# Where the residual is added in a graph-network kernel: in an accumulating output scatter, or on VectorE from a sorted copy, with other lead times in the plan

## The chip, the cores and the metric

The kernel runs on one core of one Trainium2 chip. The metric is the device time of one execution in microseconds (us). Engine names are those of the profile: PE is TensorE (PEld its weight loads), DVE is VectorE, ACT is ScalarE, POOL is GpSimd and SP is the engine whose queue issues the plain transfers.

## The reference

Sixteen graphs of 1024 nodes with 64 channels go through two layers. The first normalises each node's channels, multiplies by the dense adjacency matrix divided by its row sums, and adds the result to `x`. The second thins each node's list of neighbours, takes three quantiles over the remaining neighbours channel by channel (a sort of each list), passes the weighted sum through two small matrix products and adds that.

```python
h = jnp.maximum(_layernorm(x, axis=-1), 0.0)
x = x + _L0_gnn_ref(h, adj)                    # (adj / row sums) @ h
h = jnp.maximum(_layernorm(x, axis=-1), 0.0)
x = x + _L1_gnn_ref(h, adj, nodemask, W1, b1, W2, b2)

# inside _L1_gnn_ref
adj_d = _dilate_adj(adj, mask)                 # drops some neighbours
agg = _weighted_nanquantile_agg(x, adj_d > 0)  # quantiles 0.25, 0.5, 0.75
out = x + agg
h = relu(out @ W1 + b1)
y = h @ W2 + b2
return y * mask[..., None]
```

## The kernel before

The first layer works graph by graph. Eight row blocks of 128 nodes are loaded (`at`), their signs taken on ACT (`sg`), neighbours listed on DVE (`rec`), the blocks transposed on PE (`pt`, copied to `att`) and multiplied with the normalised nodes (`products`). The result, the input plus the messages, lies in the tile `row` in its columns from `X1`. The stream `channels` normalises it, stores it with SP to the output `out` (line 708) and the normalised channels to a table `tab` in DRAM. The stream `endings` sorts the nodes by the length of their lists: each of eight indirect DMAs per graph scatters 128 rows of `row`, without the part from `X1`, to their sorted places in `srt` in DRAM (line 775).

Four graphs make a group of 32 tiles of 128 nodes with lists of like length. One `Job` takes a class of tiles: lists of 15, 10, 8, 7 (two tiles), 6, 5 (four), 4 (four), 3 (six), 2 (six) and 1 (five). It gathers each neighbour's channels from `tab` with one indirect DMA per tile and list place (`places`, four buffers), loads the nodes' own channels from `srt` into `S`, sorts the places on DVE in place and in PSUM (`other`), weighs them (`prod`, two buffers), and then runs `layers`: PE transposes and adds the weighted places (`pt`), ACT copies (`ot`), PE multiplies by `W1` (`ph`), ACT applies the bias and relu (`hid`), PE multiplies by `W2` and adds the second bias by a product with a row of ones (`py`), and ACT multiplies by the mask (`y`). At most four tiles share one `py`, so that there are 56 such groups in the whole kernel. Last, one indirect DMA per tile adds 128 rows of `y` to the output in DRAM (line 1012). The very long lists of the first tile of each group are done together by `long_lists`, with up to 88 gathers per tile (`lplaces`), as four more jobs. So there are 16 x 8 = 128 row scatters (`srt<-row`) and 128 output scatters (`out_dram<-y`).

The order of work on DVE and POOL is written out when the program is built, by the class `Plan`. The work is a set of generators. Each yields the engine that it needs next and a time at which its operands should be there, and the plan picks the one that can begin first by its own prices. These times only set the order of instructions: on the chip each engine takes its queue in order and waits for semaphores. Margins are added to the operands' times:

```python
BREATH = 0.8
AHEAD = 16
SLACK = 2.0
LOOSE = 7.0
```

An indirect DMA costs 1.27 us in the plan, whatever it does, and its data are ready 2.2 us later (line 292); a memset on POOL costs 0.15. Every scatter that directly follows one of the same kind is preceded by a memset of `turn` (line 788). `room(name, bufs)` is the time at which the oldest buffer of a tile comes free. Of the program's engines only DVE and POOL keep the plan's order by hand; the tile framework orders the others. If a list is longer than its class allows, a flag `go` starts a dense path instead, which these inputs don't need.

Of the kernel before, what the change touches and what calls it, by code (L numbers as in the profile page):

```python
# [9 lines left out]
F32 = mybir.dt.float32  # L10
# [4 lines left out]
AF = mybir.ActivationFunctionType  # L15
OP = mybir.AluOpType
AX = mybir.AxisListType

P = 128
# [192 lines left out]
AHEAD = 16  # L212
SLACK = 2.0
LOOSE = 7.0


class Timed:
# [13 lines left out]
class Plan:  # L231
# [24 lines left out]
    def room(self, name, bufs):  # L256

        tiles = self.slots.get(name, ())
        if len(tiles) < bufs:
            return 0.0  # L260
        old = tiles[-bufs]
        return INF if self.users[old] else max(self.used.get(old, 0.0), self.ready.get(old, 0.0))

    def at(self, *tiles):
        return max(self.ready.get(t.tensor.name, INF) for t in tiles)
# [98 lines left out]
def list_path(ctx, tc, x, adj, nodemask, w1, b1, w2, b2, out, go):  # L364
# [9 lines left out]
    W = C + 2  # L374
    PW = W // 2
    REC = 8 * NSEG + 2
    R0 = W
    X1 = RW = R0 + REC
    NTAU = N // SUB
    NF = NG + NG + len(LONG)  # L380

# [58 lines left out]
    nc.sync.dma_start(w2_sb, w2)  # L440
    b1_sb = consts.tile([H, 1], F32, name="b1_sb")
    nc.sync.dma_start(b1_sb, b1.rearrange("(h o) -> h o", o=1))
    b2_sb = consts.tile([1, CO], F32, name="b2_sb")
    nc.sync.dma_start(b2_sb, b2.rearrange("(o c) -> o c", o=1))
    taus = consts.tile([P, len(QUANTILES)], F32, name="taus")
    for k, (tau, wt) in enumerate(QUANTILES):
        nc.vector.memset(taus[:, k:k + 1], tau)
# [107 lines left out]
    def beginnings(pool, now):  # L555

        for b, st in enumerate(batch):
            now[0] = b
            yield "DVE", lambda: max(known(st, "xt", "mrow"), room("h0", 3), room("row", 4))
            mrow_f = new(tiny, [NT, P], F32, "mrow_f", 2)  # L560
            nc.vector.tensor_copy(mrow_f, st["mrow"])

            h0 = new(pool, [P, NT, C + 1], F32, "h0", 3, users=2)
            nc.vector.memset(h0[:, :, C:], 1.0)
            row = st["row"] = new(pool, [P, NT, X1 + C], F32, "row", 4, users=1)
            nc.vector.memset(row[:, :, C:W], -1.0)
            yield from normed(h0[:, :, :C], st["xt"])
            st["h0"] = h0
            yield "PE", lambda: max(at(mrow_f), room("ps_small", 3))
            pm = new(ps_s, [P, HALF], F32, "ps_small", 3, users=1)  # L570
            nc.tensor.transpose(pm[:, :NT], mrow_f, ident[:NT, :NT])
            yield "ACT", lambda: at(pm)
            nc.scalar.copy(row[:, :, RW - 1], pm[:, :NT])
            nc.scalar.copy(row[:, :, RW - 2], row_f)
            free(pm)
# [79 lines left out]
    def products(pool, now):  # L655


        for b, st in enumerate(batch):
            now[0] = b
            for hf in range(2):  # L660
                yield "PE", lambda: INF if st["copied"][hf] < 2 * BPH else max(
                    at(st["att"][hf]), known(st, "h0"), room("ps_small", 3)
                )
                po = new(ps_s, [P, HALF], F32, "ps_small", 3, users=1)
                for q in range(NT):
                    if q and q % 2 == 0:
                        yield "PE", always
                    nc.tensor.matmul(
                        po[:C + 1, :], st["h0"][:, q, :], st["att"][hf][:, q, :],
                        start=(q == 0), stop=(q == NT - 1),  # L670
                    )
                free(st["att"][hf])
                free(st["h0"])
                yield "ACT", lambda: max(at(po), room("msg", 2))
                msg = new(pool, [C + 1, HALF], F32, "msg", 2)
                nc.scalar.copy(msg, po[:C + 1, :])
                free(po)
                yield "PE", lambda: max(at(msg), room("ps_small", 3))
                pb = new(ps_s, [P, HALF], F32, "ps_small", 3, users=1)
                sums = pb[:, :BPH * (C + 1)].rearrange("p (k c) -> p k c", c=C + 1)  # L680
                for k in range(BPH):
                    nc.tensor.transpose(
                        sums[:, k, :], msg[:, k * P:(k + 1) * P], ident[:C + 1, :C + 1]
                    )
                yield "DVE", lambda: at(pb) + SLACK
                x1 = st["row"][:, hf * BPH:(hf + 1) * BPH, X1:]
                deg = new(tiny, [P, BPH], F32, "deg", 2)
                nc.vector.tensor_scalar(deg, sums[:, :, C], 1.0, None, op0=OP.max)
                nc.vector.reciprocal(deg, deg)
                nc.vector.tensor_tensor(  # L690
                    x1, sums[:, :, :C], deg.unsqueeze(2).to_broadcast([P, BPH, C]), OP.mult
                )
                nc.vector.tensor_tensor(
                    x1, x1, st["xt"][:, hf * BPH:(hf + 1) * BPH, :], OP.add
                )
                free(pb)
                st["residual"] += 1
            free(st["xt"])

    def channels(pool, now):  # L700

        for b, st in enumerate(batch):
            now[0] = b
            row = lambda: st["row"]
            yield "DVE", lambda: known(st, "row") if st["residual"] == 2 else INF
            yield from normed(row()[:, :, :C], row()[:, :, X1:])

            nc.sync.dma_start(out[b].rearrange("(t p) c -> p t c", p=P), row()[:, :, X1:])
            nc.sync.dma_start(
                tab[b * TS:b * TS + N, :].rearrange("(t p) w -> p t w", p=P), row()[:, :, :W]  # L710
            )
            st["normed"] = True

    def endings(pool, now):

        first = lambda rank: rank - 3000
        for b, st in enumerate(batch):
# [53 lines left out]
            to = new(pool, [P, NT], I32, "to", 2)  # L771
            nc.vector.scalar_tensor_tensor(to, low, float(1 - GB), pos, op0=OP.mult, op1=OP.add)
            for t in range(NT):
                yield "POOL", lambda: max(at(to), at(row)) + LOOSE if "normed" in st else INF, first
                scatter(srt[g], row[:, t, :RW], to[:, t:t + 1], sorts[g])
            free(row)
            progress["batches"] = b + 1

# [4 lines left out]
            in_offset=bass.IndirectOffsetOnAxis(ap=idx, axis=0),  # L783
        )

    def scatter(dst, src, idx, others, op=OP.bypass):
        if plan.last is others:
            nc.gpsimd.memset(turn, 0.0)
        ins = nc.gpsimd.indirect_dma_start(
            out=dst, out_offset=bass.IndirectOffsetOnAxis(ap=idx, axis=0),  # L790
            in_=src, in_offset=None, compute_op=op,
        )

        for other in others:
            tc.declare_no_dep(ins.ins, other, reason="rows of their own")
        others.append(ins.ins)
        plan.last = others

    class Job:
# [8 lines left out]
        def run(self):  # L808
# [9 lines left out]
            progress["ahead"] += T * (n - 1)  # L818
            if short:
                mine = self.S  # L820
                self.S = new(pool, [P, T, W], F32, "S", 4, users=1)
                nc.sync.dma_start(self.S, mine)
            for t in range(T):
                for k in range(n - 1):
                    if t or k:
# [2 lines left out]
                    gather(A[:, k + 1, t, :], self.table, self.idx[:, t, k:k + 1])  # L828
                    progress["ahead"] -= 1
            yield "DVE", lambda: max(  # L830
                at(A, self.S) + SLACK, room("prod", 2) if short else 0.0,
                room("other" if short else "long_other", 1),
            ), self.later
            yield from self.sort()
# [129 lines left out]
        def layers(self, terms, sources):  # L964

            T, R = self.T, terms[0][0].shape[1]
            yield "PE", lambda: max(at(*sources) + LOOSE, room("y", 4), room("pt", 2))
            y = new(mlp, [P, T, CO], F32, "y", 4, users=1)
            for t0 in range(0, T, 4):
                ts = range(t0, min(t0 + 4, T))  # L970
                M = len(ts) * P
# [23 lines left out]
                yield "PE", lambda: max(at(hid) + SLACK, room("ps_small", 3))  # L995
                py = new(ps_s, [P, HALF], F32, "ps_small", 3, users=1)
                pv = py[:, :len(ts) * CO].rearrange("p (t c) -> p t c", c=CO)
                for i, t in enumerate(ts):
                    nc.tensor.matmul(
                        pv[:, i, :], hid[:, i * P:(i + 1) * P], w2_sb, start=True, stop=False  # L1000
                    )
                    nc.tensor.matmul(pv[:, i, :], ones_f[:1, :], b2_sb, start=False, stop=True)
                yield "ACT", lambda: at(py) + SLACK
                for i, t in enumerate(ts):
                    nc.scalar.activation(
                        y[:, t, :], pv[:, i, :], AF.Copy, scale=self.mask[:, t:t + 1]
                    )
                free(py)
            for t in range(T):
                yield "POOL", lambda: at(y) + LOOSE  # L1010
                rows = out_rows[:min(self.g + 1, NG) * GB * N, :]
                scatter(rows, y[:, t, :], self.nodes_i[:, t:t + 1], scatters, OP.add)
            free(y)
            progress["jobs"][self.g] += 1

    def group(g):
# [107 lines left out]
        for i, ts in enumerate(classes):  # L1124
            n, T = CAPS[ts[0]] + 1, len(ts)
            sl = slice(ts[0], ts[-1] + 1)
            job = Job(
                gat, n, T, keys[:, sl, :n - 1], idx[:, sl, :], node[:, sl], mask[:, sl],
                nodes_i[:, sl], table, tiles[:, sl, :W], g,
            )  # L1130
            plan.add(job.run(), 100 * g + i)
        progress["groups"] = g + 1
# [393 lines left out]
```

## Time and profile before

| what | value |
|---|---|
| median of 3 runs | 1586.0 us (1583.88 to 1586.02) |
| the profiled execution | 1823.34 us |
| its span | 1821.4 us |
| TensorE clock granted in it | 0.653 |
| busy in the span: DVE, POOL, PE, ACT | 1240.1, 1050.8, 825.6, 609.3 us |

A group of the profile names the output and the inputs of an instruction by the program's names, its shapes and count, its busy time and the mean of one. After the bar stands the idle time of the engine just before those instructions and what ended it. "issue" is idle time in which the profile shows nothing that was waited for. Nearly all instructions carry line 225, that of a helper which records every operation for the plan, so tiles tell them apart. For an indirect DMA the POOL time is that of the instruction on POOL; the data move on the DMA engines beside it.

### The profile page before, as it was taken

How to read it: one execution, taken by the hardware profiler on the slowest of the kernel's cores; microseconds unless marked ns; L12 is line 12 of the kernel's file. 1: busy time of each engine (PE TensorE's matmuls, PEld its weight loads, DVE VectorE, ACT ScalarE, POOL GpSimd, SP SyncE). 2: the span in 40 equal slices, each digit the busy share in tenths (PEclk: the TensorE clock that was granted, in tenths of full speed). 3: DMA queues.
4: the chain of work that ended last, by engine and by line, in shares of the span. 5: the costliest groups of instructions: out<-in, count | busy, mean ns of one | idle time of the engine just before them, and what ended most of it. 6: DMA issues, size and time to landing. Idle time of an engine off the chain costs nothing. (4 is left out here: it accounts for less than half of the span.)

```text
span 1821.4 us, 15210 instructions
## 1 busy us (share of the span) xinstructions
PE 825.6 (45%) x3336; PEld 533.0 (29%) x3336; DVE 1240.1 (68%) x4046; ACT 609.3 (33%) x1874; POOL 1050.8 (58%) x1144
## 2 busy tenths in 40 slices
PE   5767822365686572563685000110031366253364
PEld 3333411233444341232354000100021245242343
DVE  7865858475788486678642889339497678896622
ACT  8877653245655464444442000000010111010011
POOL 0112263636467655555758766567656788575757
PEclk8978855675798675775885555555555567555656
DMA  5544741233444353353222211101111112111112
GB/s 170 163 133 122 199 125 31 48 101 81 121 134 112 58 134 91 90 138 73 56 48 49 43 43 34 23 17 22 28 24 28 18 26 20 23 30 23 24 18 17
DMA packets 147941, 124.89 MB, mean 69 GB/s; under 512 B 117715, under 2 KB 117843, under 8 KB 147843
## 3 DMA queue, kind: packets, MB, share of 16 engines
q1 hardware_dynamic: 102818, 86.58, 16.8%
q0 software_dynamic: 45024, 37.28, 12.2%
q14 instruction: 71, 0.57, 0.1%
q8 instruction: 28, 0.46, 0.1%
HBM read 104.51 MB, written 19.28 MB: 68 GB/s over the span
## 5 line engine op out<-in xcount | busy, mean ns | idle before, releaser
L225 POOL DMA_INDIRECT places<-tab,idx x496 | 495.0, 998 | 165.1 <-issue 140.2
L225 PE MATMUL pt<-ident,prod 128*128 128x128 f32 (+1 forms) x736 | 161.8, 384 | 569.4 <-DVE prod L225 294.5
L225 POOL DMA_INDIRECT out_dram<-y,nodes_i x124 | 208.0, 1678 | 186.8 <-ACT y L225 127.4
L225 PEld LDWEIGHTS pt<-ident,prod 128*128 128x128 f32 (+1 forms) x736 | 134.2, 267 | 605.3 <-issue 389.7
L225 POOL DMA_INDIRECT srt<-row,to x128 | 129.4, 1011 | 259.0 <-ACT row L225 223.5
L225 PE MATMUL pt<-ident,at 128*128 128x128 f32 x1024 | 190.0, 334 | 179.6 <-ACT att L225 72.1
L225 PE MATMUL ps_small<-att,h 128*65 128x512 f32 x512 | 259.0, 652 | 17.7 <-ACT h L225 10.3
L225 PEld LDWEIGHTS pt<-ident,at 128*128 128x128 f32 x1024 | 143.5, 171 | 236.5 <-ACT att L225 97.7
L225 POOL DMA_INDIRECT lplaces<-tab,lidx x163 | 171.0, 1049 | 49.7 <-issue 49.1
L225 ACT COPY att<-pt 128x512 f32<-128x512 f32 x256 | 142.9, 583 | 155.7 <-remote 84.2
L225 DVE MAX8 rec<-sg 128x8 f16<-128x256 f16 x512 | 180.1, 414 | 9.5 <-remote 5.2
L225 ACT ACTIVATE wu<-wu 128x39 f32<-128x39 f32 (+9 forms) x40 | 9.4, 234 | 431.7 <-DVE wu L225 168.8
L225 ACT ACTIVATE sg<-at 128x1024 f16<-128x1024 f32 x128 | 134.9, 1055 | 31.7 <-DMA at<-in_adj_dram 15.3
L225 DVE TENSOR_TENSOR sg<-sg,keyed 128x1024 f16<-128x1024 f16 x128 | 87.4, 683 | 65.5 <-issue 33.4
L225 PEld LDWEIGHTS ps_small<-att,h 128*65 128x65 f32 x512 | 75.4, 153 | 149.4 <-issue 126.5
L225 ACT COPY ot<-pt 128x128 f32<-128x128 f32 (+3 forms) x56 | 22.4, 400 | 246.7 <-remote 128.2
L225 PE MATMUL ps_small<-ot,w_sb 128*128 128x128 f32 (+3 forms) x112 | 55.9, 593 | 104.7 <-ACT ot L225 72.6
L225 PE MATMUL ps_small<-w_sb,hid 128*128 128x64 f32 x256 | 72.5, 376 | 52.6 <-ACT hid L225 25.1
L225 DVE TENSOR_TENSOR other<-places,other 128x64 f32<-128x64 f32 (+6 forms) x204 | 69.5, 341 | 35.6 <-remote 16.3
L225 PEld LDWEIGHTS ps_small<-w_sb,hid 128*128 128x128 f32 x256 | 53.6, 258 | 80.5 <-ACT hid L225 40.3
L225 DVE TENSOR_TENSOR rem<-places,recs 128x30 f32<-128x30 f32 (+9 forms) x40 | 7.3, 182 | 101.7 <-DMA places<-tab,idx 90.0
L225 POOL MEMSET turn<- 128x1 f32 x204 | 76.2, 373 | 0.1
(206 smaller groups left out, 1712.2 us busy)
## 6 DMA issues: line engine op xcount, KB each, us to landing
at<-in_adj_dram SPq DMA_DIRECT2D x128, 512.0 KB
places<-tab,idx POOLq DMA_INDIRECT x496
tab<-row SPq DMA_DIRECT2D x16, 264.0 KB
xt<-in_x_dram SPq DMA_DIRECT2D x16, 256.0 KB
out_dram<-row SPq DMA_DIRECT2D x16, 256.0 KB
lplaces<-tab,lidx POOLq DMA_INDIRECT x163
recs<-srt SPq DMA_DIRECT2D x4, 544.0 KB
srt<-row,to POOLq DMA_INDIRECT x128
```

The costliest lines, as they stand in the source:

```text
L225: ins = getattr(self._engine, op)(*args, **kwargs)
```

## The change

The sorted rows now carry the first layer's result as well: `row` is laid out as channels, two markers, `x1`, and then the list record, and all of it is scattered to `srt` (656 bytes a row instead of 400). The store of `out` in `channels` goes. In `layers`, a short job loads the tiles' `x1` from `srt` into `y` (five buffers instead of four) at its start; a long job has it in its own `S`. The second bias goes into PSUM with one product for up to four tiles, ahead of the products with `W2`. The step from `py` to `y` moves from ACT to DVE, which multiplies by the mask and adds `x1` in one instruction a tile. The output scatter becomes a plain one.

In the plan, the new DVE step stands 7 us behind `py` (ACT's stood 2 behind), the output scatters 15 us behind `y` (7 before), the sort of a job 7 us behind its gathers and `S` (2 before), and the row scatters of all graphs but the first four 15 us behind their operands (7 before). `S` of a short job holds 64 columns instead of 66.

```diff
+WIDE = 15.0
...
-    R0 = W
-    X1 = RW = R0 + REC
+    X1 = W
+    R0 = X1 + C
+    RW = R0 + REC
...
-    b2_sb = consts.tile([1, CO], F32, name="b2_sb")
-    nc.sync.dma_start(b2_sb, b2.rearrange("(o c) -> o c", o=1))
+    b2_sb = consts.tile([1, 4 * CO], F32, name="b2_sb")
+    for k in range(4):
+        nc.sync.dma_start(b2_sb[:, k * CO:(k + 1) * CO], b2.rearrange("(o c) -> o c", o=1))
...
-            nc.sync.dma_start(out[b].rearrange("(t p) c -> p t c", p=P), row()[:, :, X1:])
...
-                yield "POOL", lambda: max(at(to), at(row)) + LOOSE if "normed" in st else INF, first
-                scatter(srt[g], row[:, t, :RW], to[:, t:t + 1], sorts[g])
+                yield "POOL", lambda: max(at(to), at(row)) + (LOOSE if b < GB else WIDE) if "normed" in st else INF, first
+                scatter(srt[g], row[:, t, :], to[:, t:t + 1], sorts[g])
...
-            in_=src, in_offset=None, compute_op=op,
+            in_=src, in_offset=None,
...
-                self.S = new(pool, [P, T, W], F32, "S", 4, users=1)
-                nc.sync.dma_start(self.S, mine)
+                self.S = new(pool, [P, T, C], F32, "S", 4, users=1)
+                nc.sync.dma_start(self.S, mine[:, :, :C])
+                self.residual = mine[:, :, X1:R0]
...
-                at(A, self.S) + SLACK, room("prod", 2) if short else 0.0,
+                at(A, self.S) + LOOSE, room("prod", 2) if short else 0.0,
...
-            yield "PE", lambda: max(at(*sources) + LOOSE, room("y", 4), room("pt", 2))
-            y = new(mlp, [P, T, CO], F32, "y", 4, users=1)
+            yield "PE", lambda: max(at(*sources) + LOOSE, room("y", 5), room("pt", 2))
+            y = new(mlp, [P, T, CO], F32, "y", 5, users=1)
+            x1 = y
+            if self.short:
+                nc.sync.dma_start(x1, self.residual)
+            else:
+                x1 = self.S[:, :, X1:R0]
...
+                nc.tensor.matmul(
+                    py[:, :len(ts) * CO], ones_f[:1, :], b2_sb[:, :len(ts) * CO],
+                    start=True, stop=False,
+                )
                 for i, t in enumerate(ts):
                     nc.tensor.matmul(
-                        pv[:, i, :], hid[:, i * P:(i + 1) * P], w2_sb, start=True, stop=False
+                        pv[:, i, :], hid[:, i * P:(i + 1) * P], w2_sb, start=False,
+                        stop=(i == len(ts) - 1),
                     )
-                    nc.tensor.matmul(pv[:, i, :], ones_f[:1, :], b2_sb, start=False, stop=True)
-                yield "ACT", lambda: at(py) + SLACK
+                yield "DVE", lambda: at(py) + LOOSE
                 for i, t in enumerate(ts):
-                    nc.scalar.activation(
-                        y[:, t, :], pv[:, i, :], AF.Copy, scale=self.mask[:, t:t + 1]
+                    nc.vector.scalar_tensor_tensor(
+                        y[:, t, :], pv[:, i, :], self.mask[:, t:t + 1], x1[:, t, :],
+                        op0=OP.mult, op1=OP.add,
                     )
...
             for t in range(T):
-                yield "POOL", lambda: at(y) + LOOSE
-                rows = out_rows[:min(self.g + 1, NG) * GB * N, :]
-                scatter(rows, y[:, t, :], self.nodes_i[:, t:t + 1], scatters, OP.add)
+                yield "POOL", lambda: at(y) + WIDE
+                scatter(out_rows, y[:, t, :], self.nodes_i[:, t:t + 1], scatters)
...
-                nodes_i[:, sl], table, tiles[:, sl, :W], g,
+                nodes_i[:, sl], table, tiles[:, sl, :R0], g,
```

More of the change, by code (lines that the diff above doesn't have):

```diff
@@ L564, in beginnings @@
             nc.vector.memset(h0[:, :, C:], 1.0)
-            row = st["row"] = new(pool, [P, NT, X1 + C], F32, "row", 4, users=1)
+            row = st["row"] = new(pool, [P, NT, RW], F32, "row", 4, users=1)
             nc.vector.memset(row[:, :, C:W], -1.0)
@@ L685, in products @@
                 yield "DVE", lambda: at(pb) + SLACK
-                x1 = st["row"][:, hf * BPH:(hf + 1) * BPH, X1:]
+                x1 = st["row"][:, hf * BPH:(hf + 1) * BPH, X1:R0]
                 deg = new(tiny, [P, BPH], F32, "deg", 2)
@@ L705, in channels @@
             yield "DVE", lambda: known(st, "row") if st["residual"] == 2 else INF
-            yield from normed(row()[:, :, :C], row()[:, :, X1:])
-            nc.sync.dma_start(out[b].rearrange("(t p) c -> p t c", p=P), row()[:, :, X1:])
+            yield from normed(row()[:, :, :C], row()[:, :, X1:R0])
             nc.sync.dma_start(
@@ L784, in gather, with scatter @@
         )
-    def scatter(dst, src, idx, others, op=OP.bypass):
+    def scatter(dst, src, idx, others):
         if plan.last is others:
```

## The prediction

> **What bounds the kernel now.** I read the stage table first (busy us of each engine in a stretch, with instruction counts), because the kernel has two halves. Up to about 1000 us the first layer runs on all engines; after it only the second layer's gathers, sorts and small matmuls are left.
>
> ```profile
> 0.00:1000.00 1000.00, 596.29 (x2365) 352.18 (x2365) 675.77 (x2255) 547.43 (x1675) 496.70 (x608) 0.73 0.40 104
> 1000.00:1822.00 822.00, 229.33 (x973) 180.79 (x972) 564.31 (x1791) 61.87 (x199) 554.13 (x537) 0.56 0.16 26
> ```
>
> Columns after the width: PE, PEld, DVE, ACT, POOL, TensorE clock, DMA share, GB/s. In the second half DVE (564) and POOL (554) look equally loaded, and DMA (0.16) and ACT (62) are out of it. So I asked for POOL's groups in that stretch alone (busy, mean ns, then the idle time just before them).
>
> ```profile
> L225 POOL DMA_INDIRECT places<-tab,idx x241 | 244.8, 1016 | 74.6 <-issue 66.4 <-DMA places<-tab,idx 4.6 <-DMA tab<-drop,didx 1.4
> L225 POOL DMA_INDIRECT lplaces<-tab,lidx x163 | 171.0, 1049 | 49.7 <-issue 49.1 <-DMA lplaces<-tab,lidx 0.6
> L225 POOL DMA_INDIRECT out_dram<-y,nodes_i x70 | 120.4, 1720 | 110.4 <-ACT y L225 77.2 <-ACT prod L225 21.1 <-issue 11.2
> L225 POOL DMA_INDIRECT out_dram<-y,lnodes_i x4 | 6.5, 1626 | 5.3 <-ACT wu L225 4.4 <-issue 0.9
> ```
>
> A fixed gap ("issue") follows each gather, so 404 gathers occupy POOL's queue for 244.8+171.0+74.6+49.7 = 540 us. The 74 output scatters hold it for 127 busy + 12 issue = 139 us, and for 77.2+21.1+4.4 = 103 us more POOL stands at a scatter whose `y` isn't there, with the next gathers queued behind it. Together 782 of 822 us: POOL's queue, waits included, is full. DVE isn't: of its 258 idle us these three are the waits for gathers, 118 us.
>
> ```profile
> DVE rem L225 <- DMA places<-tab,idx: 80.3, 8, 25.0
> DVE lrem L225 <- DMA lplaces<-tab,lidx: 26.9, 1, 26.9
> DVE rem L225 <- issue: 11.1, 3, 8.5
> ```
>
> POOL in order of time shows the price of one scatter and one wait near the end (start, us, [idle before]), and the plain scatters of rows at the first half's end:
>
> ```profile
> 1742.99 1.50 POOL L225 DMA_INDIRECT places<-tab,idx  x1 [0.30 <-issue]
> 1756.50 1.62 POOL L225 DMA_INDIRECT out_dram<-y,nodes_i  x1 [12.01 <-ACT y L225]
> 1795.46 1.57 POOL L225 DMA_INDIRECT out_dram<-y,nodes_i  x1 [0.19 <-issue]
> 1797.34 1.57 POOL L225 DMA_INDIRECT out_dram<-y,nodes_i  x1 [0.19 <-issue]
> ...
> 980.80 0.97 POOL L225 DMA_INDIRECT srt<-row,to  x1 [0.19 <-issue]
> 981.77 0.12 POOL L225 MEMSET turn<- 128x1 f32 x1
> 982.08 0.96 POOL L225 DMA_INDIRECT srt<-row,to  x1 [0.19 <-issue]
> ```
>
> Start to start, an accumulating scatter takes 1797.34-1795.46 = 1.88 us, a plain one 982.08-980.80 = 1.28 us, each with its memset. The planner (line 292) prices both alike, at 1.27 + 0.15.
>
> **What the Trainium skill says.** "Perfetto Trace Analysis", section "DMA Instruction — SWDGE (GPSIMD)": the end of such an instruction is the last descriptor written, not the data's arrival. So 1.57 against 0.97 is work on POOL itself; the trace agrees, since the next POOL instruction starts right after it. "DMA: Bandwidth & Descriptors", section "Rules for kernel authors": an accumulating DMA reads its destination and writes it later, and must wait for other accesses of those bytes. The kernel before does so (the `out` store ahead of the scatters); no wait for that store appears in POOL's list, so dropping it is worth nothing by itself. "Perfetto Trace Analysis", section "Optimizing Scalar/DVE Operations": about 125 ns fixed for DVE on PSUM, 60 on SBUF. The trace has 424 ns for 128x256 from PSUM (`row<-ps_small,deg`) and 430 from SBUF (`row<-row,xt`): no such difference in the profiled durations.
>
> **The change part by part** (us of the profiled execution, which took 1823.3 with a span of 1821.4; the median of the runs is 1586.0, so a saving is scaled by 0.87. The profiled execution is slower by 237 us, and no view says where).
>
> 1. *Plain instead of accumulating scatters.* 74 in the second half x (1.88-1.28) = 44. The last 17 are bound by `y` in the end: it is ready at 1805.3 and the last scatter starts at 1812.4, 7 to be won of 10, so 41. The 54 in the first half free 54x0.60 = 32 of POOL, where it waits for ACT and DVE anyway (in 200 to 1000 us 78 for `row`, 50 for `y`, 24 for `nodes_i`): taken 0, ends 0 and 32.
>
> 2. *Scatters planned 15 instead of 7 us behind `y`.* Only the order on POOL changes: more gathers stand ahead of each scatter, none waits on purpose. The 13 waits of the second half are 10.6, 12.9, 14.0, 7.2, 12.3, 4.4, 10.5, 5.7, 11.3, 12.0, 1.5 and two near nothing. Eight us off each leaves 28 of 103, so 75 at most. But `y` now passes DVE's queue, planned 7 us behind its PSUM tile, and what is late there stays late: I take half, 37; ends 0 and 103. Late next are DVE's step on `py` and the sorts behind it.
>
> 3. *Bias once per group.* 256 bias records of 379 ns become 112 wider ones (56 groups; 128x256 records elsewhere take 580 ns). It moves ahead of `hid`, where PE stands idle, and for four tiles 4x0.62 = 2.5 us leave the path to `y` (pairs start 0.62 apart at the clock of 0.5). Against waits that item 2 cut already: 5; ends 0 and 20.
>
> 4. *Last step on DVE.* No row has a scalar_tensor_tensor of 128x64 from PSUM. Nearest is tensor_tensor `other<-S,places` 128x64 with PSUM output, about 0.22 us; the page's 125 ns plus 64/0.96 = 67 ns gives an estimate of 0.19. I take 0.23, ends 0.15 and 0.31 (ACT's time for it). Second half: 74x0.23 = 17, hidden in DVE's gather waits but for 4; cover gone, 23. First half: 54x0.23 = 12 on the busiest engine: 6 lost, ends 0 and 17. ACT loses 128x0.313 = 40 us; it is off the path in the second half, so 0 taken, up to 10 gained in the first.
>
> 5. *The new wait on DVE.* Behind a step on `py` stand sorts, and in the first half also the layer norms and the listing; `room("places")` makes POOL wait for those sorts. First half: POOL's 7 waits for `y` there came to 50; if all pass to DVE, 50 are lost, if the planned 7 us hold, 0. I take 8. The second half's share is in item 2, and its extreme is the rival below.
>
> 6. *SP.* 16 stores of 0.43 go, 40 loads of `x1` into `y` of 0.37 come, and 3 bias loads of about 0.38 ahead of the first `at`: 1 lost at the start. A load of `y` waits for the scatter of five jobs ago and holds back `at` loads behind it; they run up to five tiles ahead: 0 taken, ends 0 and 15 lost.
>
> 7. *Sorts 5 us and late row scatters 8 us further back.* Both change only order. The first can take 5 us from each of the 12 gather waits (118) while POOL stays the bound: 0 taken, ends 20 gained, 10 lost. The second could delay the last group's start by its 8 us; gathers of group 2 cover that: 0, ends 10 gained, 8 lost.
>
> 8. *Wider sorted rows* (656 instead of 400 bytes). Gathering `adj` rows of 4096 bytes takes POOL 1.00 us, of 264 bytes 0.94 to 1.0, so its time doesn't follow bytes; the DMA share leaves room: 0.
>
> Sum: 41 + 37 + 5 - 4 - 6 - 8 - 1 = **64**. 1823.3 - 64 = 1759.3, or 0.9649; times 1586.0 is **1530**.
>
> **The rivals.**
> *Everything lines up:* with scatters costing what the planner assumes, POOL no longer slips behind it, and all 103 us of waiting go; half of the 32 counts too. 41+103+16+5 less 15 for DVE is 150, scaled 131: **1455**. For it: the waits are of the size of the slip, 74x(1.88-1.42) = 34 us by the end. Against: PE runs at half clock, slower than planned.
>
> *DVE becomes the bound (slower):* the wait for `y` moves onto it. Its slot lies 7 us behind `py`, POOL's lay some 9 behind it, so the same 13 waits would cost 103+13x2 = 129. Second half: 564 busy + 17 + 129 + its 140 idle us that have nothing to do with gathers = 850 against 822, even if no gather is ever late; with 20 lost in the first half, 48, scaled 42: **1628**. It decides from where DVE's waits for `py` and gathers together pass 822-564-17-140 = 101 us. Against it: the planner places that step 7 us late where ACT's had 2, and ACT's order, which often held `ot` up behind `wu`, gets shorter.
>
> *The change gives back what it gains:* POOL empties sooner but `places` has four buffers, and the sorts that release them come later: **1586**. Against it: in the list of waits no gather waits long for a sort (6.1 us is the longest).
>
> **How the numbers follow.** 0.2% (3 us) is about what a measurement of this kernel can tell from no change. POOL's queue shortens: 0.58, own range 1490 to 1570 (items 2 and 5 between a quarter and three quarters of their ends). All waits go: 0.18. DVE the bound: 0.17. Given back: 0.07, of which 0.03 faster, 0.03 same, 0.01 slower. Faster 0.79, same 0.03, slower 0.18. Leaving out the best third of the second case and half of the third, the range is 1440 to 1605.
>
> **What would show it.** Right: the output scatter at 0.97 us and a start-to-start of 1.28; POOL's waits at it under 60 us after 1000; the second half some 70 us shorter, the first within 20. Item 4 is right if the new DVE group has 0.15 to 0.31 us. DVE's idle time before it tells item 5: under 60 us in all for my case, over 100 in the second half for the slower one. Wrong altogether if the scatter keeps its 1.6 us, or if the first half grows by over 30.

## The result and the profile after

The changed kernel took 1579.08 us (median of six runs, 1575.99 to 1583.16), the kernel before beside it 1585.32 (six runs, 1583.88 to 1587.35). The ratio is **0.9962**, with a 95% interval of 0.9946 to 0.9977: a gain of 6 us, where 56 were forecast.

The same program runs at one of two paces: on five chips the kernel before took 1587 to 1589 us and on three others 1851 to 1856, so every ratio below is against runs of the kernel before beside it, and traces are compared at one pace only. The timed runs above are of the first pace. The profile that the prediction was read from (1823 us) was of the second. For the comparison I therefore use another profiled execution of the kernel before, of 1587.6 us (span 1585.7); the changed kernel's has a span of 1576.7.

First the groups of the page that the change touches: busy us, mean ns, then idle time before. The kernel before:

```profile
L225 POOL DMA_INDIRECT out_dram<-y,nodes_i x124 | 207.5, 1673 | 68.2 <-ACT y L225 35.0
L225 POOL MEMSET turn<- 128x1 f32 x204 | 76.5, 375 | 0.1
L225 ACT ACTIVATE y<-ps_small,recs 128x64 f32<-128x64 f32 x124 | 31.3, 313 | 88.3 <-PE ps_small L225 88.1
```

The changed kernel:

```profile
L226 POOL DMA_INDIRECT out_dram<-y,nodes_i x124 | 128.9, 1039 | 55.3 <-DVE y L226 20.2
L226 DVE SCALAR_TENSOR_TENSOR y<-ps_small,recs,y 128x64 f32<-128x64 f32 x124 | 28.2, 275 | 61.7 <-PE ps_small L226 61.7
```

The store did become cheap: 1039 instead of 1673 ns, and POOL's busy time fell from 1061.8 to 980.5 us. But DVE now stands idle for 61.7 us in front of its new step, until the matmul (`py`, in `ps_small`) is done. Before, ACT waited there, for 88.1 us.

The stretch from 800 us to the end, where only the second layer is left, in the table by stage (PE, PEld, DVE, ACT, POOL). Before:

```profile
800.00:1600.00 800.00, 244.24 (x1052) 194.14 (x1052) 571.18 (x1816) 70.21 (x223) 591.65 (x576) 0.57 0.20 29
```

After:

```profile
800.00:1600.00 800.00, 212.25 (x966) 167.21 (x966) 591.39 (x1902) 50.45 (x141) 545.21 (x583) 0.57 0.16 32
```

The kernels end at 1585.7 and 1576.7, so the stretch is really 785.7 and 776.7 us long. POOL is relieved by 46 us in it, DVE loaded by 20. DVE is idle for 785.7 - 571.2 = 214.5 us before and 185.3 after. What it waits for there, before:

```profile
DVE rem L225 <- DMA places<-tab,idx: 62.8, 7, 20.7
DVE lrem L225 <- DMA lplaces<-tab,lidx: 38.7, 2, 36.1
DVE rev L225 <- DMA srt<-row,to: 21.4, 1, 21.4
```

And after (us in total, times, longest):

```profile
DVE y L226 <- PE ps_small L226: 61.4, 16, 7.3
DVE lrem L226 <- DMA lplaces<-tab,lidx: 55.7, 1, 55.7
DVE rem L226 <- DMA places<-tab,idx: 15.9, 2, 9.6
```

The waits for POOL's short gathers shrink from 62.8 to 15.9 us. The faster POOL alone doesn't do that: in the run with plain stores alone, below, they are still 55.5. Two others take their place: 61.4 us for the matmul behind the last step, and one wait of 55.7 us in place of 36.1 for the gathers of the very long lists. The sum of what is shown hardly moves, 123 before and 133 after; the rest of DVE's idle time falls from 92 to 52, of which 16 us are one wait of 16.9 us for `go` that shrinks to 0.5.

### The profile page after: what moved, and what is told of

The parts are those of the page before. It is cut to its first block, busy times and chain, and to the rows that moved or that the text cites. A ratio compares the mean times of both kernels' runs of the same rounds, so it can differ in the third digit from the quotient of the medians.

```text
span 1576.7 us, 14919 instructions
## 1 busy us (share of the span) xinstructions
PE 749.9 (48%) x3192; PEld 470.5 (30%) x3192; DVE 1262.8 (80%) x4174; ACT 577.2 (37%) x1746; POOL 980.5 (62%) x1144
## 5 line engine op out<-in xcount | busy, mean ns | idle before, releaser
L226 POOL DMA_INDIRECT places<-tab,idx x496 | 502.1, 1012 | 155.9 <-issue 145.5
L226 PE MATMUL pt<-ident,at 128*128 128x128 f32 x1024 | 173.3, 316 | 84.7 <-ACT att L226 50.9
L226 PEld LDWEIGHTS pt<-ident,at 128*128 128x128 f32 x1024 | 133.6, 161 | 134.1 <-ACT att L226 77.4
L226 POOL DMA_INDIRECT out_dram<-y,nodes_i x124 | 128.9, 1039 | 55.3 <-DVE y L226 20.2
L226 DVE SCALAR_TENSOR_TENSOR y<-ps_small,recs,y 128x64 f32<-128x64 f32 x124 | 28.2, 275 | 61.7 <-PE ps_small L226 61.7
L226 DVE TENSOR_TENSOR places<-places,other 128x64 f32<-128x64 f32 (+2 forms) x208 | 62.4, 309 | 4.9
L226 DVE TENSOR_TENSOR long_other<-lplaces 128x512 f32<-128x512 f32 (+5 forms) x124 | 63.6, 554 | 0.4
L226 DVE TENSOR_TENSOR lplaces<-long_other 128x512 f32<-128x512 f32 (+7 forms) x116 | 61.1, 566 | 0.1
L226 PE MATMUL ps_small<-ot,w_sb 128*128 128x128 f32 (+3 forms) x112 | 51.6, 550 | 16.1 <-ACT ot L226 14.8
```

The lines of the kernel that those rows point to most:

```text
L226: ins = getattr(self._engine, op)(*args, **kwargs)
```

## The experiments

**Theory.** The gain of the cheaper store was real, and was given back on DVE: its last step, planned 7 us behind its matmul, comes to the head of DVE's queue too early and stops the sorts behind it. **Rivals.** The store's time on POOL was never on the path. The loads of the layer-1 term into `y` block SP's queue and make the last group late. The planned lead times of the sorts, row scatters and stores made a worse order.

**Repeats.** The changed kernel once more, and the kernel before for its profile at the timed runs' pace.

> The kernel after, unchanged, in a session of its own. The first session of experiments found the kernel before at 1851 us, where the comparison of before and after had 1585. Theory S (a session runs at one of two paces, and the first profile of before came from a slow one): if before is again near 1850 here, after is near its own slow pace, and the ratio shows what the change is worth there, below 0.96 if the forecast's mechanism holds at that pace; if before is near 1585, after is near 1579. Rival (the profiled before was slow by chance of that execution): before 1585 and after 1579 whatever the session.

> The kernel before, unchanged, profiled in the same session as e5. If the session runs at the pace of 1585 us, this is the profile that the forecast lacked: waits of POOL for y well under the 180 us of the first profile, and no waits of DVE for itself. If it runs at 1850, the profile is the first one again.

1579.62 us against 1588.78, ratio 0.9944 [0.9929, 0.9959]; the kernel before 1587.6 under the profiler. The small gain holds. This execution was profiled too, so a profile need not cost the 237 us by which the one shown first exceeded the timed runs.

**Plain stores alone.** In the kernel before:

```diff
-                scatter(rows, y[:, t, :], self.nodes_i[:, t:t + 1], scatters, OP.add)
+                scatter(rows, y[:, t, :], self.nodes_i[:, t:t + 1], scatters, OP.bypass)
```

> The kernel before with plain output stores and nothing else changed, same order of instructions on every engine (the layer-1 term is left out of the output); where the kernel before takes about 1587 us. Theory A, the stores' GpSimd time is worth most of its saving also in the old order: the 74 stores after 817 us give 0.6 us each, 44 us, of which VectorE's waits for gathered rows (102 us there) can take most: 1545 to 1560. Theory B, without a new order the saving is taken by what waits elsewhere, the last group's start and the matmuls: 1575 to 1590. At the slower pace it is measured at a ratio of 1.011.

1548.64 us against 1589.29, ratio **0.9742** [0.9699, 0.9785]. One word gives 40.7 us, with the plan's order untouched. From its trace:

```profile
L225 POOL DMA_INDIRECT out_dram<-y,nodes_i x124 | 133.2, 1074 | 85.9 <-ACT y L225 46.0
```

POOL's busy time falls by 81 us to 980.8, and half of it arrives at the end. Theory A's range holds, and the rival that POOL was never on the path falls. It also follows that the rest of the change *costs*: 1548.6 + 31 = 1579.6. In this run's second half DVE is busy for 564.4 us of 744.8 and idle for 180.4.

**The lead of DVE's last step.** In the changed kernel, one line, first to 15 us and then to 2:

```diff
-                yield "DVE", lambda: at(py) + LOOSE
+                yield "DVE", lambda: at(py) + WIDE
```

> The changed kernel with VectorE's last step planned 15 instead of 7 us behind the matmul that it reads. Where the kernel before takes about 1585 us and the changed one 1579: theory A, VectorE's waits for the matmuls (66 us in all in the changed kernel, 61 of them after 800 us) are on the path, so that most of them go: 1579 - 61 = 1518 us at best, 1550 if half are taken by what is late next. Theory B, they take the place of other waits of VectorE, for gathered rows, and the end is set by the last group's late start: 1570 to 1590. Where the kernel before takes about 1855 and the changed one 1992: theory A 1930 to 1970, theory B 1980 to 2010.

**1520.86 us** against 1588.80, ratio **0.9571** [0.9541, 0.9601], close to the best that theory A allowed. DVE's waits after 800 us:

```profile
DVE y L226 <- PE ps_small L226: 28.8, 8, 8.7
DVE lrem L226 <- DMA lplaces<-tab,lidx: 23.9, 1, 23.9
DVE rev L226 <- DMA srt<-row,to: 18.7, 1, 18.7
DVE rem L226 <- DMA places<-tab,idx: 18.7, 4, 7.5
```

The last steps' wait is halved. The long lists' falls by 32 us as well, but by another way: in the order that this lead makes, the last group's records are loaded earlier (see the loads into `y` below). DVE's idle time after 800 us is 714.0 - 578.9 = 135.1 us, 50 less than in the changed kernel, and the span is 63 us shorter. The other direction, with `SLACK` (2 us) in that line:

> The changed kernel with VectorE's last step planned 2 instead of 7 us behind its matmul: the other direction of the run with 15 us, which gave 1521. Theory A, the step's waits for the matmul set the time: they grow from 66 to some 100 us and the kernel takes 1595 to 1625 where the one before takes about 1588. Theory B, the run with 15 us was another lucky order and the lead itself decides nothing: anything from 1520 to 1600, the waits no longer than 66 us. Where the kernel before takes about 1855 and the changed one 1992, A says 1990 to 2020, B 1900 to 2000.

1588.52 us against 1587.74, ratio 1.0007 [0.9993, 1.0021].

```profile
DVE y L226 <- PE ps_small L226: 119.3, 21, 13.1
DVE lrem L226 <- DMA lplaces<-tab,lidx: 25.3, 1, 25.3
DVE rem L226 <- DMA places<-tab,idx: 8.6, 1, 8.6
```

The wait doubles, as theory A says, yet the time is 6 us under its range. The last group's records go out at 857.5 us in this order, 29 us earlier than in the changed kernel, and the long lists cost 25 instead of 56 us. So the lead sets the wait, in order 28.8, 61.4 and 119.3 us for 15, 7 and 2. What a microsecond of it costs isn't isolated: 33 us less came with 63 us less of span, 58 us more with 8 us more, because each lead also makes another order. Of the 63 us of span that the lead of 15 brought, 33 (61.4 - 28.8) lie in the wait itself, 32 in the long lists' gathers and 12.5 in DVE work that is done before 800 us; other waits grow by some 15.

The path can be followed back from the last output scatter but one, through whatever ended each wait. After 800 us it runs over PE (the transposes and matmuls of `layers`, which the last step waits for) for 36 us with the lead of 15, for 72 with 7 (89 in the repeat) and for 145 with 2; in the kernel before it was 88. So this wait is on the path. But in the changed kernel the path also runs over POOL for 287 us and over DVE for 244 (255 and 273 in the repeat), so neither queue sets the length alone.

**The loads into `y`.** In the changed kernel the layer-1 term isn't loaded into `y` for the short jobs and the identity matrix's first columns are added in its place; the plan still prices the load.

```diff
-                nc.sync.dma_start(x1, self.residual)
+                plan.note("SP", "dma_start", (x1, self.residual), {})
...
-                    nc.vector.scalar_tensor_tensor(
-                        y[:, t, :], pv[:, i, :], self.mask[:, t:t + 1], x1[:, t, :],
-                        op0=OP.mult, op1=OP.add,
+                    args = y[:, t, :], pv[:, i, :], self.mask[:, t:t + 1], x1[:, t, :]
+                    plan.note("DVE", "scalar_tensor_tensor", args, {})
+                    tc.nc.vector.scalar_tensor_tensor(
+                        *args[:3], ident[:, :C] if self.short else args[3], op0=OP.mult, op1=OP.add
```

> The changed kernel without the 40 transfers of the layer-1 term into y (a constant is added instead; the layer-1 term is left out of the output of the short jobs), same order on GpSimd; where the kernel before takes about 1588 us and the changed one 1579. Between 815 and 887 us the last group's records stand in SyncE's queue behind transfers that wait 18 us in all for stores of y and 37 and 8 us for VectorE. Theory A, the y transfers make the late start: the records go out some 18 us earlier and the time falls to 1560 to 1568. Theory B, the order of the plan makes it (the queue waits for VectorE in any case): 1575 to 1582. Where the kernel before takes about 1855 it is measured at 1970 and 1986, and nothing new is expected.

1566.58 us against 1587.38, ratio 0.9860 [0.9819, 0.9901]. Against the changed kernel's 0.9944 that is 0.84% or 13 us: A, at its weak end. What SP's queue waits for from 822 to 892 us, in the changed kernel:

```profile
SPq L226 <- DVE other L226: 36.6, 1, 36.6
SPq L226 <- DMA out_dram<-y,nodes_i: 18.0, 5, 11.5
SPq L226 <- DVE gone L226: 8.4, 1, 8.4
```

The last group's records (`recs`) stand at the end of these three. They go out at 886.7 us; in the kernel before it was 835.8. Without the loads it is 876.7, and DVE's wait for the long lists is still 55.6 us. So the loads make 10 of the 51 us, and their 13 us of time don't come by way of the long lists: by the traces, 7 us more of DVE's work is done before 800 us and 8 us less of idle time stands behind it. Whether the loads cost by their waits or as transfers, the run doesn't tell. The rest of the 51 us is SP's in-order queue behind a load of `S`, which waits for a sort on DVE, and the records' own wait for DVE. In the order with a lead of 15 the records come ahead of those and go out at 820.9, with the loads into `y` in place.

**At the other pace.** The remaining runs fell where the kernel before takes 1851 to 1856 us. They can be read against each other, not against the numbers above. The kernel before again:

> The kernel before, unchanged, profiled a second time. Theory P (the profile's 237 us of extra time belong to profiling this kernel, not to the kernel): the profiled execution is again near 1820 us (1780 to 1860) while the plain run stays at 1585. Rival Q (the first profiled execution happened to be disturbed): the profiled execution comes near 1590 us and its POOL waits for y fall well under the 180 us of the first profile.

1844.8 us. Plain stores alone, three times:

> The kernel before with one word changed: the output scatter stores instead of adding, so the first layer's result is missing from the output. Order, plan and all waits are as before. Theory P (the 0.6 us more per accumulating scatter hold POOL only a little, since POOL's queue is not what bounds the plain run): 1575 to 1590 us, within 10 us of before. Rival R (the plain scatter gives what was forecast, 40 us and more, and the new DVE step or the plan take it back): 1530 to 1550 us. The profile of this run should show the output scatter at about 0.97 us in both; under P its profiled execution tells whether the accumulating scatters are what makes profiling slow (1585 then) or not (1820).

> The kernel before with the output scatter storing instead of adding (the first layer's result is then missing from the output), in another session: where before took 1851 us this kernel said nothing on the pace of 1585. Order and waits are as before. The profile of before at the fast pace has POOL busy with these scatters for 214 us, of which 77 are the accumulation, and its waits for y are down to 44. If POOL's queue is still what bounds the second half: 1540 to 1560 us. If DVE and POOL share it, the gain is smaller: 1560 to 1580. If it is hidden: 1583 to 1592.

> The kernel before with plain instead of accumulating output stores, same order of instructions (the layer-1 term is left out of the output). Theory A, the cheaper store is worth the whole gain of the second half: 1585 - 74 x 0.6 = 1541 us at most, 1570 if only the waits of VectorE and ScalarE for GpSimd's data shrink (ratio 0.97 to 0.99). Theory B, GpSimd's time isn't on the path that sets the end: 0.998 to 1.002. At the slower pace both are measured already at 1.011.

1.0115 [1.0074, 1.0156], 1.0109 [1.0057, 1.0161] and 1.0107 [1.0027, 1.0187]: less work in the same order is slower there by 1%. The kernel before with the later lead times alone (`WIDE` at stores and late row scatters, `LOOSE` at sorts):

```diff
...
-                at(A, self.S) + SLACK, room("prod", 2) if short else 0.0,
+                at(A, self.S) + LOOSE, room("prod", 2) if short else 0.0,
...
-                yield "POOL", lambda: at(y) + LOOSE
+                yield "POOL", lambda: at(y) + WIDE
```

> The kernel before with the change's three lead times alone: output scatters 15 us behind y, sorts 7 us behind gathers, row scatters of graphs 4 to 15 15 us behind their operands. The accumulating scatter and ACT's last step stay. If the forecast's item 2 holds (waits of POOL for y fall by half): 1545 to 1560 us. If order hardly matters because the waits of the first profile were a product of profiling: 1575 to 1592 us. If later sorts hold buffers longer: 1592 to 1610 us.

1.0223 [1.0183, 1.0262]. The changed kernel as it is:

> The changed kernel itself, as the yardstick of the runs beside it. If the chip runs the kernel before in about 1585 us, both theories expect 1579 (ratio 0.994 to 0.998). If it takes about 1850, the changed kernel hasn't been timed at that pace: the theory that the gain lies in GpSimd's waits, which are longer there, expects a ratio near 0.99; the theory that at that pace any cheaper store disturbs the order (as with plain stores alone, 1.011) expects 1.01 to 1.03.

1960.68 and 1979.07 us, with two further runs at 2005 and 2006, against 1855.67. The ratio, of the first two, is **1.0629** [1.0530, 1.0729]. At this pace the change is a loss. The changed kernel with all four lead times as before (7 us for stores and row scatters, 2 for sorts and DVE's step), twice:

> The kernel after with all four lead times set back (2 us for the sorts and the DVE step, 7 us for both scatters); plain stores, DVE step, x1 from the sorted rows stay. If the DVE step waits for PE and its 7 us are what keeps that small: slower than after, 1590 to 1620 us. If the lead times are worth nothing: 1575 to 1583 us. If they cost: 1555 to 1575 us.

> The kernel after with its four lead times set back as in e4, in another session. At the fast pace: slower than after (over 1590 us) if the lead times carry the gain; 1575 to 1585 if they are worth nothing; 1550 to 1572 if they are what takes the gain of the plain scatters back.

1.0283 [1.0244, 1.0321] and 1.0331 [1.0278, 1.0383]: about half of that loss comes with the lead times. The row scatters' lead alone put back to 7 us, twice:

```diff
-                yield "POOL", lambda: max(at(to), at(row)) + (LOOSE if b < GB else WIDE) if "normed" in st else INF, first
+                yield "POOL", lambda: max(at(to), at(row)) + LOOSE if "normed" in st else INF, first
```

> The kernel after with the row scatters alone planned 7 us behind their operands again. In the trace of after the last group's list (recs) is loaded at 891 us, of before at 836, and POOL then waits 27 us for its node numbers. If the later row scatters push the last group back in the plan: recs before 870 us and 1545 to 1570 us. If SP's queue does it (theory of e10): recs stays near 890 and 1575 to 1585.

> The changed kernel with the row scatters planned 7 instead of 15 us behind their operands again. Theory A (SyncE's queue): within 8 us of the changed kernel. Theory B (the plan's order delays the last group): the last group starts some 10 to 50 us earlier, 1530 to 1570. Theory C, the planner's order answers to small changes without a rule: anything up to 3% to either side.

1.0708 [1.0652, 1.0764] and 1.0713 [1.0637, 1.0788], so this lead isn't the cause. And without the loads into `y`, as above, twice:

> The kernel after with one kind of transfer left out: the 40 loads of x1 into y are not issued, and DVE adds a constant tile instead (so x1 is missing from the short jobs' output). The plan still prices the load, so DVE and POOL keep after's order. In after, SP stands for y's buffer, that is for an output scatter, 431 us in 39 waits, and recs and S stand behind it. If that takes back the gain: 1540 to 1570 us and recs before 870. If SP's waits are covered: 1575 to 1583.

> The changed kernel without the 40 transfers of the layer-1 term into y (a constant is added instead; the layer-1 term is left out of the output of the short jobs), with the same order on GpSimd. Theory A, the transfers in SyncE's queue wait for the stores and hold back the last group's records and neighbour lists behind them, which start 55 us later: about 1579 - 50 = 1530 us. Theory B, the late start comes from the order in the plan: no change, 1575 to 1582.

1.0650 [1.0578, 1.0722] and 1.0698 [1.0620, 1.0776], no gain either. Which of the sorts', the stores' and DVE's lead loses at this pace was not separated: with DVE's lead of 2 the waits for its matmul are longer there too (150.5 us, against 69.1 on the same chip with the row scatters' lead alone put back, apart from 60 and 15 us that the traces give to no named instruction), and still that kernel is faster. So the explanation by this wait is one for the pace of the timed runs and not for the other.

## Why the prediction failed

The direction was right, the size was not: 1579 against 1530. The second half became 9 us shorter, where some 70 were named as the sign of being right.

*Item 1, plain stores: right.* Forecast 41, or 36 scaled; measured alone 40.7. The price of 0.60 us less from start to start holds. POOL in order of time near the end of the kernel before, at the timed runs' pace:

```profile
1559.78 1.57 POOL L225 DMA_INDIRECT out_dram<-y,nodes_i  x1 [0.19 <-issue]
1560.74 0.72 POOL L225 MEMSET turn<- 128x1 f32 x1
1561.65 1.57 POOL L225 DMA_INDIRECT out_dram<-y,nodes_i  x1 [0.19 <-issue]
```

And of the changed kernel:

```profile
1554.17 0.96 POOL L226 DMA_INDIRECT out_dram<-y,nodes_i  x1 [0.19 <-issue]
1555.12 0.11 POOL L226 MEMSET turn<- 128x1 f32 x1
1555.43 0.96 POOL L226 DMA_INDIRECT out_dram<-y,nodes_i  x1 [0.19 <-issue]
```

That is 1.26 us against 1.87. (One reading was loose: it isn't the next POOL instruction that starts after the accumulating scatter's end. The memset starts 0.96 us after the scatter's start, before that end; the next scatter starts after it.) The reading that POOL's queue bounds the second half fits too, in that half of the time taken off POOL came off the whole.

*Item 5, the new wait on DVE: the step that failed.* It was priced at 8 us for the first half, where the trace has one wait of 3.6; the second half got no price of its own and went into item 2. There the trace has 61.4 us, just over the 60 that the prediction named as the limit for its case. The working took the planned 7 us as cover, but on the chip DVE waits for the matmul up to 7.3 us more; more lead halves the wait, less doubles it. Each of these waits holds the sorts behind it, and an SP load can stand behind a sort (36.6 us above). POOL's gathers don't: in POOL's list they wait 0.3 us for sorts.

Not all of the 61.4 us is loss. Beside the run with plain stores alone, the changed kernel is 31.9 us longer by span: DVE has 25.1 us more work (1262.8 against 1237.7), and after 800 us it is idle for 185.3 us against 180.4. So the wait stands in good part where waits for gathers stood (15.9 against 55.5), and what failed with it is the hiding of item 4: of the new step's work 10 us were taken as lost, and by this account all 25 are. Only with the lead of 15, where DVE is idle for 135 us, is the added work covered.

*Item 2, stores later in the plan: mis-sized.* It gave 37 of the 64 us and rested on 103 us of POOL waits for `y`. At the pace of the timed runs there were 17.4 + 9.0 = 26.4 us after 800 us. POOL's groups from there on, in the kernel before:

```profile
L225 POOL DMA_INDIRECT out_dram<-y,nodes_i x79 | 132.1, 1673 | 40.7 <-ACT y L225 17.4 <-issue 13.2 <-ACT prod L225 9.0
```

And in the changed kernel:

```profile
L226 POOL DMA_INDIRECT out_dram<-y,nodes_i x79 | 83.7, 1060 | 31.3 <-DVE y L226 13.6 <-issue 12.6 <-DVE places L226 1.7
```

After the change 13.6 are left of them, and 3.2 at the scatters of the long lists. So at most 26 us were there to be had, and about ten went. The same effect alone was not run at this pace.

*Scaling by 0.87.* The prediction noted that no view said where the 237 us between the profile and the runs lay, and scaled all items alike. They were not spread evenly. Part of them lay in late starts on DVE (last section), and POOL's waits for `y` were longer there: 148.5 us in the whole profile that was read, 44.0 at the pace of the timed runs. The item that stood on durations of instructions scaled well; the one that stood on waits did not.

*Item 6, SP's loads: inside its bounds, wrongly placed at 0.* They cost 13 us of the 15 allowed. *Item 7, lead times of sorts and row scatters: the outcome that it named happened by another way.* (Its 118 us of gather waits include 11.1 us, "issue", for which the trace names nothing.) The last group's records start 51 us later, not 8. Its last row scatter is not late (811.6 us against 826.9 before); the records stand in SP's queue behind a transfer that waits for a sort.

*Item 4, the size of the step:* 275 ns where 230 were taken, inside the bounds. *Item 8:* row scatters of wider rows have a median of 960 ns against 967, right at 0. *Item 3*, the bias, was not isolated.

*The rivals.* "DVE becomes the bound" had the mechanism and twice the size: 129 us of waits for `py` forecast, 61.4 found. In its terms the second half is 591 busy + 133 for `py` and gathers + 52 other idle = 777. Busy and idle time make up the length on every engine, so this sum doesn't show that DVE sets it; the path above runs over POOL as well. It does show why the kernel isn't slower than before: the 140 us of other idle time that the rival assumed are 52 at this pace. "Given back" (1586, at 7 in a hundred) was nearest in size, though its mechanism, POOL waiting for sorts to release `places`, is not what the trace shows.

What remains open: with the lead of 15 the rest of the change is worth 1548.6 - 1520.9 = 28 us beside the store, and how these divide between relieved ACT, the bias and the later stores was not tested. The rival of the other lead times (sorts, row scatters, stores) was run at the other pace alone, so for the timed runs it stays open. So does how much of the 58 us between the leads of 7 and 15 is the wait itself and how much the other order.

## What to carry to other kernels

When a step moves to the engine with the most work, its wait for the operand moves too and stops everything queued behind it there: price that wait, count the step's work as lost until something is shown to cover it, and try more lead in a hand-made order before judging the change. If a profile's span is far from the timed runs, its waits are not the runs' waits: take durations of instructions from it, and treat savings of waits as unknown until a profile at the right pace is there. In an in-order transfer queue, look at what a late group's first load stands behind.

## What was not expected of the hardware

At the slower pace the instructions of VectorE and ScalarE take as long as at the other (busy 1240.5 against 1237.7 us and 609.9 against 607.5 for the kernel before; PE has 836.8 against 787.2); on VectorE nearly all of the 257 us between the two profiles is idle time. A VectorE step that waits only for VectorE steps ahead of it starts within 0.05 us at the faster pace, in all of 2053 cases. From VectorE in order of time at the slower pace (start, us, [idle before]):

```profile
349.92 0.30 DVE L225 TENSOR_TENSOR other<-places,other 128x128 f32<-128x128 f32 x1 [1.18 <-DVE places L225]
351.32 0.30 DVE L225 TENSOR_TENSOR other<-places,other 128x128 f32<-128x128 f32 x1 [1.10 <-DVE other L225]
352.71 0.30 DVE L225 TENSOR_TENSOR other<-places,other 128x128 f32<-128x128 f32 x1 [1.10 <-DVE other L225]
```

The same kind of steps at the faster pace, four in a row:

```profile
301.42 1.28 DVE L225 TENSOR_TENSOR other<-places,other 128x128 f32<-128x128 f32 x4
```

Counted over the whole trace, 69 of 2054 such hand-overs are later than 0.9 us at the slower pace, 120 us in all, and none at the faster; the profile that the prediction was read from has 67, with 114 us. Most come in stretches of 5 to 40 us. GpSimd is in an indirect transfer for 61% of this idle time, but for 56% of the whole span too, so that doesn't point to it.

The cause stays open. One difference can be seen in the recording: the traces at the slower pace hold about half as many semaphore updates (12544 for the kernel before, against 24227). Part of their waits therefore has no name, and whether the slower pace belongs to the chips, to their recording or to the session isn't known; each chip was seen in one session. It does mean that a change to this kernel can gain in one session and lose in another: 0.9944 and 1.0629 for this one.
